# A transformer block on one Trainium2 core: the output projection adds PSUM to its own partial sums, with three steps put in another order

## The chip, the cores and the metric

The kernel runs on one core of one Trainium2 chip. The metric is the time of one execution on the device, in microseconds (us), of that core. Five engines appear in the profile: TensorE (PE, with its weight loads as PEld), VectorE (DVE), ScalarE (ACT), GpSimd (POOL) and SyncE (SP), which here only issues DMAs. [...]

## The reference

The input x has 32 sequences of 64 tokens and 1024 features, float32. The reference computes

```python
x = x + attn(cond(x))     # cond: x @ W.T plus a rank-32 term chosen per sequence
x = x + ffn(cond2(x))     # two layers of 8 gated rank-16 experts beside a dense product
```

where `attn` is causal attention with 32 query heads, 8 key and value heads of width 32, rotary positions, and an output projection `out @ w_o.T + b_o` with a 1024 x 1024 weight. Only `w_o`, its bias and the sum with x are touched by the larger part of the change.

## The kernel before, in words

**The two stages.** The weights of consecutive layers are first multiplied with each other (`multiply`, L530): the chain called cq multiplies `w1` into the query weights, then ckv, then cf. After about 297 us the tokens are done in two halves of 1024 (`for hf in range(2)`, L766): query and key products, scores and values, output projection, and then the feed-forward part. Both halves run the same code, so each stage around the change comes twice.

**The products.** A product of a 256-column weight chunk with 1024 columns is a `Group` (L220): a 2 x 2 block scheme with seven block products in place of eight. It needs sums of weight blocks (`weight_sums`, L163, on POOL) and sums of columns (`column_sums`, L176, on DVE, called t1 to t4 below). The seven steps are p1, p6, p5, p7, p2, p4 and p3, on three PSUM banks: x (p1, then p2), y (p6, then p7, then p4) and z (p5, then p3). Three partial sums go to SBUF tiles: p1 is copied by ACT (L273), and two DVE additions follow p6 (L279, "u1") and p7 (L291, "u2"). A step that accumulates onto a bank has to wait until the partial result before it has been read from there: p7 until u1 is read from y, p4 until u2 is read from y, p3 until the result called out11 is read from z. The four results of a group are out11, out00, out10 and out01, in the order in which their products end.

**The output projection.** `o_pairs` (L1011) makes its groups. `known` (L1018) is called as soon as each of the three partial sums exists and lets POOL add it to x; `out_o` (L1022) then lets DVE add the PSUM bank to x, in the same x tile, so that this DVE instruction (L1026, or L1028 without a bias) waits for the POOL instruction (L1020) that was given to x before it. Half of the projection (G = 0, four groups) is done between the attention units u = 4 to 7; the other half (G = 1) follows in two pairs.

**The attention units.** A unit u has four score tiles. `scores` (L873) makes them on PE, `masked` (L899) lets DVE add the mask into a tile e, `maxima` (L908) takes row maxima on DVE and subtracts them on POOL (L913), `normalised` (L915) lets ACT take exponentials, DVE sum them and take reciprocals (L922, L923), and POOL multiply (L925). `turned` (L927) transposes e on PE, and `values` (L939) multiplies with v.

**What sets the order.** Within `tc.manual_schedule()` (L1034) the order of each engine's queue is the order of the calls in the code. In the loop at L1092 an iteration for u is: transposes, p1, `normalised(u + 1)` (after p6 if u is 4), the scores of unit u + 2, p6, their four mask additions, p5, p2, p7, two maxima, the values, out11, p4, two maxima, p3. In the loop at L1038, which goes on with the query products beside the first two units, an iteration is p1, p6, `masked(u)` (which makes its scores first), p5, and so on. Outside of such a block (the feed-forward part, which begins at L1142) a planner with estimated costs picks the order from what it expects to be ready.

**The first loads.** SP issues the first loads of chain cq at L568 to L576: for the first half of the inner dimension the weight chunk `w0`, four chunks of `wq` with `b1` after the first, then `w1`; then the same for the second half. The first product needs `w0[:, :4, :128]` and the first 512 columns of `wq` for chunks 0 to 3. DVE makes t1 and t2 chunk by chunk in turn, then t3 (L579).

Of the kernel before, what the change touches and what calls it, by code (L numbers as in the profile page):

```python
# [16 lines left out]
ALU = mybir.AluOpType  # L17
AX = mybir.AxisListType

P = 128  # L20
D = 1024
KC = D // P
B, S = 32, 64
# [53 lines left out]
def block_kernel(ctx: ExitStack, tc: tile.TileContext, a, out: bass.AP):  # L77
    nc = tc.nc
# [27 lines left out]
    mask = cst[:, _C["mask"]]  # L106
# [19 lines left out]
    bqk, bo, bb = biases[:, 0:10], biases[:, 10 : 10 + KC], biases[:, 10 + KC :]  # L126
# [31 lines left out]
    H = KC // 2  # L158

    def by_sequence(m):  # L160
        return m.rearrange("p (b t) -> p b t", t=S)
# [311 lines left out]
    with tc.tile_pool(name="gen", bufs=1) as gen:  # L473
# [87 lines left out]
        wq = gen.tile([P, KC, D], F32, tag="right", name="wq")  # L561
# [3 lines left out]
        b1 = gen.tile([P, KC, LR], F32, tag="b1", name="b1")  # L565
        w0, w1 = (wp.tile([P, KC, WG], F32, tag="w", name=f"w_cq{g}") for g in range(2))
        first_half, second_half = slice(0, H), slice(H, KC)
        for half in (first_half, second_half):  # L568
            nc.sync.dma_start(w0[:, half], a["w1"][0, :, half])
            for kc in range(half.start, half.stop):  # L570
                nc.sync.dma_start(wq[:, kc, :], a["wqkv"][:, kc, :D])
                if kc == 0:
                    nc.sync.dma_start(b1, a["b1"])
            nc.sync.dma_start(w1[:, half], a["w1"][1, :, half])
        nc.sync.dma_start(index, a["index"])
        nc.sync.dma_start(cst, a["consts"])  # L576
        b1q_rows = rank_rows("b1q", b1, wq, D, b1q)
        t_cq = columns("cq", gen, halves(wq, D), 512)
        for which in ((0, 1), (2,)):  # L579
            for kc in range(H):  # L580
                t_cq.make(kc, which)
        t_ckv, make_ckv = sums_of("ckv", wkv, NQ - D)
        t_cf, make_cf = sums_of("cf", w3, D)

# [181 lines left out]
    for hf in range(2):  # L766
# [3 lines left out]
        def x_half(kc, c, x=x):  # L770
            return x[kc].rearrange("p (b c t) -> p b c t", c=2, t=S)[:, :, c, :]
# [101 lines left out]
        def scores(u):  # L873
            g, b0 = u // 4, u % 4 * 4
            sc = [ps_tile(f"sc_{hf}_{u}_{j}") for j in range(4)]
            for n in range(8):
                mp, b = n // 4, b0 + n % 4
                for j in range(4):
                    rows = slice(j * HD, (j + 1) * HD)
                    nc.tensor.matmul(  # L880
                        sc[j][:, n * S : (n + 1) * S],
                        q[rows, g, b, 2 * mp : 2 * mp + 2, :].rearrange("p m t -> p (m t)"),
                        k[rows, g, b, :],
                        start=True,
                        stop=True,
                    )
            return sc
# [3 lines left out]
        units = {}  # L891

        def per_key(v):
            return v.rearrange("p (n t) -> p n t", t=S)
# [1 line left out]
        def wide(v):  # L896
            return v.unsqueeze(2).to_broadcast([P, 8, S])

        def masked(u, sc=None):  # L899
            units[u] = []  # L900
            for j, sc in enumerate(sc or scores(u)):
                e = ep.tile([P, 512], F32, tag="e", name=f"e_{hf}_{u}_{j}")
                nc.vector.tensor_add(  # L903
                    per_key(e), per_key(sc), mask.unsqueeze(1).to_broadcast([P, 8, S])
                )
                units[u].append(e)

        def maxima(u, js=range(4)):  # L908
            for j in js:
# [99 lines left out]
                column_sums(tiles, lambda i, c: b(i, c, kcs), cols)  # L1009

        def o_pairs(G, p, ws, t, banks):  # L1011
            nm = f"o{hf}{G}{p}"
            w, s = ws

            def group(i):
                g = 2 * p + i

                def known(r, c, add):  # L1018
                    xo = x_half(g + r * H, c)
                    nc.gpsimd.tensor_add(xo, xo, by_sequence(add))  # L1020

                def out_o(r, c, ps, add):  # L1022
                    xo = x_half(g + r * H, c)
                    if G == 0:
                        bias = bo[:, g + r * H : g + r * H + 1]
                        nc.vector.scalar_tensor_tensor(xo, by_sequence(ps), bias, xo, ALU.add, ALU.add)  # L1026
                    else:
                        nc.vector.tensor_add(xo, by_sequence(ps), xo)  # L1028

                return Group(f"{nm}{i}", w[:, i], s[:, i], t, out_o, None, known, banks[i])  # L1030

            return [group(i) for i in range(2)]

        with tc.manual_schedule():  # L1034

            rotated()
            pair, held = qk_pair(2), None
            for u in range(2):  # L1038
                g = pair
                g.p1()  # L1040
                g.p6()
                masked(u)
                g.p5()
                maxima(u)
                g.p7()
                g.p2()
                normalised(u)
                g.together(held)
                if u == 0:
                    held, pair = g, qk_pair(3, ps_tile)  # L1050
                else:
                    wv = load_w(cqkv[:, :, 5 * WG :], f"v{hf}")
                g.p4()
                g.p3()
            g.last_rows()
            v_ranks(0, 1)
            g.out01()
            v_mult(0)
            rotated()
            pools.close()  # L1060
            wsp = scoped(f"ws{hf}", 4)
            sums = scoped(f"sums_o{hf}")
            t0 = [sums.tile([P, 2, 512], F32, tag=f"sum{j}", name=f"sum{j}_o{hf}0") for j in range(4)]
            v_out(0)
            for u in range(4):
                first, second = 2 * u + 1, 2 * u + 2
                ws = turned(u)
                if u > 0:
                    normalised(u + 1)
                v_mult(first)  # L1070
                v_out(first)
                if 0 < u < 3:
                    o_sums(0, t0, u - 1, u)
                masked(u + 2)
                if u == 3:
                    values(u, ws, group_bank)
                    o_sums(0, t0, u - 1, u + 1)
                    maxima(u + 2)
                    break
                v_ranks(second, second + 1)  # L1080
                v_mult(second)
                maxima(u + 2)
                v_out(second)
                values(u, ws)
                if u == 0:
                    wo0 = o_load(0, 0)

            wo1 = o_load(0, 1)
            ot = Columns(o_columns(0), 512, 2, [[t[:, kc, :] for kc in range(2)] for t in t0])
            pairs = o_pairs(0, 0, wo0, ot, (group_bank, group_bank))  # L1090
            pairs += o_pairs(0, 1, wo1, ot, (group_bank, group_bank))
            for u in range(4, 8):  # L1092
                o = pairs[u - 4]
                ws = turned(u)
                o.p1()
                if 4 < u < 7:
                    normalised(u + 1)
                elif u == 7:
                    t1 = [
                        [ep.tile([P, 512], F32, tag="e", name=f"sumo{hf}{j}{kc}") for kc in range(2)]  # L1100
                        for j in range(4)
                    ]
                    o_sums(1, t1, 4, 7)
                sc = scores(u + 2) if u < 6 else None
                o.p6()
                if u == 4:
                    normalised(u + 1)
                if u < 6:
                    masked(u + 2, sc)
                o.p5()  # L1110
                o.p2()
                o.p7()
                if u < 6:
                    maxima(u + 2, range(2))
                if u == 6:
                    wo0 = o_load(1, 0)
                values(u, ws)
                o.out11()
                o.p4()
                if u < 6:  # L1120
                    maxima(u + 2, range(2, 4))
                o.p3()
            o_sums(1, t1, 7, 8)
            ot = Columns(o_columns(1), 512, 2, t1)
            wo1 = o_load(1, 1)
            pairs = o_pairs(1, 0, wo0, ot, (group_bank, ps_tile))
            pools.close()

            xt = columns(f"y{hf}", scoped(f"sums_y{hf}", side="right"), x_half, 512)
            for p in range(2):  # L1130
                for step in ("p1", "p6", "p5", "p7", "p2", "out11", "p4", "p3"):
                    for o in pairs:
                        getattr(o, step)()
                    if p == 1 and step in ("p5", "out11"):
                        xt.make(("p5", "out11").index(step))
                pairs = o_pairs(1, 1, wo1, ot, (group_bank, ps_tile))
            attention.close()
# [209 lines left out]
```

## Time and profile before

| what | value |
|---|---|
| time, median of 3 runs | 1225.39 us (1225.35 to 1227.83) |
| time of the profiled execution | 1223.48 us |
| its span, first to last instruction | 1221.7 us |
| around the span | 1.78 us |
| granted TensorE clock | 0.999 |
| busy: PE, DVE, POOL, ACT | 98%, 47%, 42%, 13% |
| output projection beside units 4 to 7, first half of the tokens | 482.41 to 548.13 us |
| the same, second half | 946.99 to 1012.69 us |

Times inside the trace count from the first instruction of the profiled execution. A line of a timeline gives the start, the duration, the engine, the source line, the operation with its output and inputs, how many were merged, and in brackets how long the engine was idle before it and what ended that. [...] products of four times two 512-column passes start 3.43 us apart although each shows 3.60 us, so stalls are read from start to start.

### The profile page before, as it was taken

How to read it: one execution, taken by the hardware profiler on the slowest of the kernel's cores; microseconds unless marked ns; L12 is line 12 of the kernel's file. 1: busy time of each engine (PE TensorE's matmuls, PEld its weight loads, DVE VectorE, ACT ScalarE, POOL GpSimd, SP SyncE). 2: the span in 40 equal slices, each digit the busy share in tenths (PEclk: the TensorE clock that was granted, in tenths of full speed). 3: DMA queues.
4: the chain of work that ended last, by engine and by line, in shares of the span. 5: the costliest groups of instructions: out<-in, count | busy, mean ns of one | idle time of the engine just before them, and what ended most of it. 6: DMA issues, size and time to landing. Idle time of an engine off the chain costs nothing.

```text
span 1221.7 us, 13568 instructions
## 1 busy us (share of the span) xinstructions
PE 1202.3 (98%) x5434; PEld 610.6 (50%) x5434; DVE 574.8 (47%) x940; ACT 153.5 (13%) x282; POOL 510.2 (42%) x437
## 2 busy tenths in 40 slices
PE   7999999999999999999999999999999999999998
PEld 2444875555444477444444444444478444444443
DVE  4312151115358789753942113457789764743111
ACT  1001000000001125320000000001124330000000
POOL 3441361443435646734726011533656752821010
PEclk9999999999999999999999999999999999999999
DMA  6563732644111111013114235111111023212110
GB/s 241 201 221 101 269 131 70 207 152 157 35 34 36 37 68 70 21 67 122 35 35 138 69 107 169 35 35 35 35 70 38 34 70 101 73 35 69 50 55 35
DMA packets 57504, 108.83 MB, mean 89 GB/s; under 512 B 5088, under 2 KB 34144, under 8 KB 56160
## 3 DMA queue, kind: packets, MB, share of 16 engines
q1 hardware_dynamic: 41648, 79.53, 19.5%
q10 hardware_dynamic: 13104, 20.03, 4.5%
q0 software_dynamic: 2688, 8.39, 2.0%
q8 instruction: 43, 0.70, 0.2%
q14 instruction: 21, 0.17, 0.0%
HBM read 83.72 MB, written 24.22 MB: 88 GB/s over the span
## 4 chain that ended last, share of the span: by engine, by line
PE 91%; DVE 4%; POOL 3%; issue 1%; DMA 0%; ACT 0%; SPq 0%; POOLq 0%; DVEq 0%; ACTq 0%
PE qk_y L249 7%; PE f_y L249 7%; PE o_y L249 5%; PE qk_z L249 5%; PE qk_x L249 5%; PE v L859 5%; PE f_z L249 5%; PE f_x L249 4%; PE o_z L249 4%; PE o_x L249 4%; PE cq_y L249 3%; PE cf_y L249 3%; PE cq_x L249 2%; PE cf_x L249 2%; PE cq_z L249 2%; PE cf_z L249 2%
## 5 line engine op out<-in xcount | busy, mean ns | idle before, releaser
L809 POOL TENSOR_TENSOR raw<-raw,consts 128x512 f32<-128x512 f32 x40 | 63.1, 1585 | 105.9 <-DVE t L808 105.9
L913 POOL TENSOR_TENSOR e<-e,top 128x512 f32<-128x512 f32 x64 | 64.9, 1042 | 55.4 <-DVE top L912 40.4
L925 POOL TENSOR_TENSOR e<-e,tot 128x512 f32<-128x512 f32 x64 | 66.2, 1064 | 20.0 <-DVE tot L923 20.0
L249 PE MATMUL qk_x<-x,w_qk 128*128 128x512 f32 x160 | 72.2, 594 | 0.0
L249 PE MATMUL qk_y<-sum_x,s_qk 128*128 128x512 f32 x160 | 72.0, 593 | 0.0
L170 POOL TENSOR_TENSOR s_f<-w_f 128x512 f32<-128x512 f32 x8 | 11.0, 1379 | 123.0 <-DMA w_f<-cffn 99.4
L249 PE MATMUL o_x<-q,w_o 128*128 128x512 f32 x128 | 58.9, 592 | 0.0
L859 PE MATMUL v<-w_v,x 128*128 128x256 f32 x256 | 58.7, 382 | 0.0
L249 PE MATMUL f_x<-x,w_f 128*128 128x512 f32 x128 | 57.9, 592 | 0.0
L249 PE MATMUL f_y<-sum_y,s_f 128*128 128x512 f32 x128 | 57.5, 592 | 0.0
L922 DVE TENSOR_REDUCE tot<-e 128x8 f32<-128x512 f32 x64 | 40.2, 665 | 25.4 <-ACT e L917 25.2
L859 PEld LDWEIGHTS v<-w_v,x 128*128 128x128 f32 x256 | 47.4, 190 | 8.4 <-issue 2.7
L1020 POOL TENSOR_TENSOR x<-x,o_u 128x512 f32<-128x512 f32 x32 | 42.0, 1322 | 22.7 <-DVE o_u L291 18.4
L249 PEld LDWEIGHTS qk_y<-sum_x,s_qk 128*128 128x128 f32 x160 | 30.3, 190 | 37.9 <-issue 37.5
L249 PEld LDWEIGHTS qk_x<-x,w_qk 128*128 128x128 f32 x160 | 30.1, 190 | 38.0 <-issue 37.9
L810 DVE TENSOR_TENSOR t<-t,consts 128x512 f32<-128x512 f32 x40 | 47.3, 1194 | 0.7
L170 POOL TENSOR_TENSOR s_qk<-w_qk 128x512 f32<-128x512 f32 x10 | 18.5, 1851 | 66.6 <-DMA w_qk<-cqkv 66.6
L917 ACT ACTIVATE e<-e 128x512 f32<-128x512 f32 x64 | 38.2, 640 | 48.9 <-POOL e L913 48.9
L903 DVE TENSOR_TENSOR e<-sc,consts 128x512 f32<-128x512 f32 x64 | 39.5, 678 | 3.2 <-PE sc L880 3.2
L249 PEld LDWEIGHTS f_y<-sum_y,s_f 128*128 128x128 f32 x128 | 24.3, 190 | 30.6 <-issue 30.6
L249 PEld LDWEIGHTS f_x<-x,w_f 128*128 128x128 f32 x128 | 24.3, 190 | 30.6 <-issue 30.6
L912 DVE TENSOR_REDUCE top<-e 128x8 f32<-128x512 f32 x64 | 39.6, 674 | 0.0
(314 smaller groups left out, 2187.9 us busy)
## 6 DMA issues: line engine op xcount, KB each, us to landing
w_qk<-cqkv SPq DMA_DIRECT2D x10, 1024.0 KB, 6.4
x<-in_xT SPq DMA_DIRECT2D x16, 512.0 KB, 7.5
w_o<-in_wo SPq DMA_DIRECT2D x16, 512.0 KB, 5.1
s_o<-wos SPq DMA_DIRECT2D x16, 512.0 KB, 6.5
w_f<-cffn SPq DMA_DIRECT2D x8, 1024.0 KB, 5.6
outT<-o ACTq DMA_DIRECT2D x32, 256.0 KB, 2.4
wq<-in_wqkv SPq DMA_DIRECT2D x8, 512.0 KB, 8.9
cqkv<-cq ACTq DMA_DIRECT2D x16, 256.0 KB, 3.8
```

Source lines behind the costliest of these rows:

```text
L170: nc.gpsimd.tensor_add(s[:, 0], a21, a22)
L249: nc.tensor.matmul(ps, self.weights[left][:, kc, :], self.right(right, kc), start=first and kc == 0, stop=kc == self.h - 1, skip_group_che ...
L809: nc.gpsimd.tensor_mul(rv, rv, c3)
L810: nc.vector.tensor_mul(t2v, t2v, s3)
L859: nc.tensor.matmul(begun[t], x[kc][:, t * P : (t + 1) * P], wv[:, kc, :], start=False, stop=kc == KC - 1, skip_group_check=True,)
L903: nc.vector.tensor_add(per_key(e), per_key(sc), mask.unsqueeze(1).to_broadcast([P, 8, S]))
L912: nc.vector.tensor_reduce(top, ev, AX.X, ALU.max)
L913: nc.gpsimd.tensor_sub(ev, ev, wide(top))
L917: nc.scalar.activation(e, e, AF.Exp, scale=SCALE)
L922: nc.vector.tensor_reduce(tot[:, i], es[i], AX.X, ALU.add)
L925: nc.gpsimd.tensor_mul(es[i], es[i], wide(tot[:, i]))
L1020: nc.gpsimd.tensor_add(xo, xo, by_sequence(add))
```

## The change

Four edits.

1. In `o_pairs`, for all groups but the last pair (`last`), DVE adds the PSUM bank (and the bias where G is 0) to the partial sum's own tile, and POOL then adds that tile to x. The three POOL additions of `known` go away there; three POOL additions after out11, out10 and out01 come in. out00, which has no partial sum, still goes straight to x on DVE.
2. In the loop over u = 4 to 7, `normalised(u + 1)` stands behind p6 for every u. Two of the four mask additions move behind p5 and p7, p7 comes ahead of p2, and out11 comes directly behind the mask additions, ahead of the values.
3. In the loop over u = 0 and 1, for u = 0 p5 comes ahead of the scores.
4. The first load of `w0` and the first of `wq` are each split into two by columns, and the first column halves of both are issued first; `b1` follows, and the second half of `w0` stands behind `w1`. DVE makes all of t1, then all of t2, then all of t3.

```diff
-        for half in (first_half, second_half):
-            nc.sync.dma_start(w0[:, half], a["w1"][0, :, half])
-            for kc in range(half.start, half.stop):
+        for r in range(2):
+            cols, outs = slice(r * D // 2, (r + 1) * D // 2), slice(r * P, (r + 1) * P)
+            nc.sync.dma_start(w0[:, first_half, outs], a["w1"][0, :, first_half, outs])
+            nc.sync.dma_start(wq[:, 0, cols], a["wqkv"][:, 0, cols])
+        nc.sync.dma_start(b1, a["b1"])
+        for half in (first_half, second_half):
+            for kc in range(max(half.start, 1), half.stop):
                 nc.sync.dma_start(wq[:, kc, :], a["wqkv"][:, kc, :D])
-                if kc == 0:
-                    nc.sync.dma_start(b1, a["b1"])
             nc.sync.dma_start(w1[:, half], a["w1"][1, :, half])
+            if half is first_half:
+                nc.sync.dma_start(w0[:, second_half], a["w1"][0, :, second_half])
...
-        for which in ((0, 1), (2,)):
+        for j in range(3):
             for kc in range(H):
-                t_cq.make(kc, which)
+                t_cq.make(kc, (j,))
...
+            last = (G, p) == (1, 1)
...
                 def known(r, c, add):
-                    xo = x_half(g + r * H, c)
-                    nc.gpsimd.tensor_add(xo, xo, by_sequence(add))
+                    if last:
+                        xo = x_half(g + r * H, c)
+                        nc.gpsimd.tensor_add(xo, xo, by_sequence(add))
...
                 def out_o(r, c, ps, add):
                     xo = x_half(g + r * H, c)
+                    bias = bo[:, g + r * H : g + r * H + 1]
+                    to, more = (xo, xo) if last or add is None else (by_sequence(add), by_sequence(add))
                     if G == 0:
-                        bias = bo[:, g + r * H : g + r * H + 1]
-                        nc.vector.scalar_tensor_tensor(xo, by_sequence(ps), bias, xo, ALU.add, ALU.add)
+                        nc.vector.scalar_tensor_tensor(to, by_sequence(ps), bias, more, ALU.add, ALU.add)
                     else:
-                        nc.vector.tensor_add(xo, by_sequence(ps), xo)
+                        nc.vector.tensor_add(to, by_sequence(ps), more)
+                    if to is not xo:
+                        nc.gpsimd.tensor_add(xo, xo, to)
...
-                masked(u)
-                g.p5()
+                if u == 0:
+                    g.p5()
+                    masked(u)
+                else:
+                    masked(u)
+                    g.p5()
...
-                if 4 < u < 7:
-                    normalised(u + 1)
-                elif u == 7:
+                if u == 7:
...
                 o.p6()
-                if u == 4:
+                if u < 7:
                     normalised(u + 1)
                 if u < 6:
-                    masked(u + 2, sc)
+                    masked(u + 2, sc, range(2))
                 o.p5()
+                o.p7()
+                if u < 6:
+                    masked(u + 2, sc, range(2, 4))
+                o.out11()
                 o.p2()
-                o.p7()
                 if u < 6:
                     maxima(u + 2, range(2))
...
                 values(u, ws)
-                o.out11()
                 o.p4()
```

`masked` takes a list of score tiles to be done (`js`), so that a unit's four mask additions can be issued in two calls.

## The prediction, on record before the changed kernel ran

> **What bounds the kernel now.** I read the page's busy times and chain first, then the list of whom TensorE waits for, then TensorE's timeline in the stages that the change touches, then DVE and POOL beside it.
>
> ```profile
> PE 1202.3 (98%) x5434; PEld 610.6 (50%) x5434; DVE 574.8 (47%) x940; ACT 153.5 (13%) x282; POOL 510.2 (42%) x437
> ...
> PE 91%; DVE 4%; POOL 3%; issue 1%; DMA 0%; ACT 0%; SPq 0%; POOLq 0%; DVEq 0%; ACTq 0%
> ```
>
> TensorE is busy nearly throughout and holds 91% of the chain that ended last. No matmul is added or removed, so all that can be won is the time in which TensorE waits. The list of its waits (total, times, longest):
>
> ```profile
> PE cq_x L249 <- DMA wq<-in_wqkv: 7.4, 1, 7.4
> PE o_y L249 <- DVE o_u L291: 2.3, 2, 1.2
> PE o_z L249 <- DVE x L1026: 1.9, 4, 0.5
> PE sc L880 <- DVE q L819: 1.1, 2, 0.5
> ```
>
> Edits 1 and 2 aim at the second and third line, edit 3 at the fourth, edit 4 at the first. TensorE in unit 4 of the first half (p7, values, p4, p3, transposes):
>
> ```profile
> 491.42 1.88 PE L249 MATMUL o_y<-sum_o,s_o 128*128 128x512 f32 x4
> 493.23 1.09 PE L948 MATMUL av<-ws,v 64*32 64x256 f32 x32
> 495.49 1.98 PE L249 MATMUL o_y<-sum_o,w_o 128*128 128x512 f32 x4 [1.16 <-DVE o_u L291]
> 498.00 1.98 PE L249 MATMUL o_z<-q,s_o 128*128 128x512 f32 x4 [0.54 <-DVE x L1026]
> 499.82 1.91 PE L933 MATMUL pt<-consts,e 128*128 128x128 f32 x16
> ```
>
> The pitch of an unhindered half product is 1.72 us (487.99 to 489.70), and 1.03 us from values to the next (512.39 to 513.41, unit 5). So p4 could start at 494.26 and started 1.23 later; p3 could start 1.81 behind p4 (1.72 and about 0.1 after a restart) and started 2.51 behind, 0.70 late. DVE shows why:
>
> ```profile
> 488.25 0.69 DVE L279 TENSOR_TENSOR o_u<-o_y,o_p 128x512 f32<-128x512 f32 x1 [1.20 <-PE o_y L249]
> ...
> 491.75 2.42 DVE L903 TENSOR_TENSOR e<-sc,consts 128x512 f32<-128x512 f32 x4
> 494.09 0.74 DVE L1026 SCALAR_TENSOR_TENSOR x<-o_x,consts,x 128x512 f32<-128x512 f32 x1
> 494.75 0.68 DVE L291 TENSOR_TENSOR o_u<-o_y,o_p 128x512 f32<-128x512 f32 x1
> ...
> 497.20 0.75 DVE L1026 SCALAR_TENSOR_TENSOR x<-o_z,consts,x 128x512 f32<-128x512 f32 x1 [0.58 <-POOL x L1020]
> ```
>
> u2 (L291), which frees y for p4, stands behind four mask additions and a result; out11 (last line), which frees z for p3, waits for POOL. POOL's queue:
>
> ```profile
> 490.66 1.27 POOL L1020 TENSOR_TENSOR x<-x,o_u 128x512 f32<-128x512 f32 x1
> 491.89 4.05 POOL L925 TENSOR_TENSOR e<-e,tot 128x512 f32<-128x512 f32 x4
> 495.89 1.27 POOL L1020 TENSOR_TENSOR x<-x,o_u 128x512 f32<-128x512 f32 x1
> ```
>
> The addition of u2 to x, for which out11 waits, sits behind four multiplications. The scores of unit 0, against those of unit 1, which nothing hinders:
>
> ```profile
> 380.68 1.34 PE L880 MATMUL sc<-k,q 32*128 32x64 f32 x40
> 382.56 0.90 PE L880 MATMUL sc<-k,q 32*128 32x64 f32 x24 [0.55 <-DVE q L819]
> 383.39 3.70 PE L249 MATMUL qk_z<-sum_x,s_qk 128*128 128x512 f32 x8
> ...
> 408.88 2.01 PE L880 MATMUL sc<-k,q 32*128 32x64 f32 x64
> 410.83 3.70 PE L249 MATMUL qk_z<-sum_x,s_qk 128*128 128x512 f32 x8
> ```
>
> 2.71 against 1.95 us to the next product: 0.76 lost.
>
> [...] the column sums L182 to L188 of two SBUF tensors take 0.69 us alone and up to 1.75 beside POOL, while L1026, with a PSUM input, took 0.75 beside POOL's multiplications. [...] the DVE addition from PSUM stays in both versions; every POOL row here reads SBUF. [...] The first product agrees: its matmuls start 0.85 us apart until about 11 us, then 0.43. [...] here two loads with 512 B rows (w_h, 572.5 to 574.5 us) ran at 275 and 347 GB/s against 413 later[...].
>
> **Edits 1 and 2, units 4 to 7.** Stalls before, start to start, p4 and p3: unit 4 1.23 and 0.70; unit 5 0 and 0.25 (513.41 to 515.38 less 1.72); unit 6 0 and 0.70; unit 7 0 and 0.24. Sum 3.12 a half; the second half has the same starts to 0.05 (p4 960.07, p3 962.57, 979.95, 995.64, 1010.87). 6.2 us in all.
>
> What is left is DVE's queue in the new order, from the start S of p6. From the trace: u1 starts at S + 2.09 (486.16 to 488.25) and takes 0.61 of pitch; four sums and two reciprocals take 2.89 (488.86 to 491.75); two mask additions 1.2; u2 0.69. So u2 ends at S + 7.5. TensorE reaches p4 at S + 8.1 (the same steps, with p7 now third): 0.6 to spare. Two more mask additions (1.2) and out11 (0.75) end at S + 9.35; p3 comes at S + 9.92: 0.55 to spare. p7, moved up, starts at S + 3.55 and needs u1, done at S + 2.8. The values' second bank needs only the first mask addition, done about S + 6.2, and comes at S + 7.1. [...] The exponentials, which ended before S + 4 in unit 4, come no later; ACT has nothing else to do between p1's copy and them; in units 5 and 6 DVE no longer waits for them (3.86 idle before L922) ahead of u1.
>
> POOL: three additions of 1.27 go, three come; out11 no longer waits for POOL. Its queue per unit stays 8 x 1.03 + 3 x 1.27 = 12.1 us in a unit of 15.3 or 17.2. The multiplications that the next transposes need end about S + 8.5 (first reciprocal S + 4.3, then 4.05), the transposes come at S + 11.65 (p4 at 8.1, p3 1.82 and the transposes 1.75 behind it): 3.2 to spare. Behind POOL's new additions stand the subtractions for the unit after the next, with 2 us or more of slack to the exponentials. In unit 7 eight column sums (5.2 us in the trace, one POOL addition beside them) run ahead of u1; p7 comes 1.7 earlier now. Unit 6's last result leaves DVE 1 us after unit 7's first transpose starts, the sums end 6.2 after it, u1 6.9; p7 comes at 6.95. That is no slack: I charge 0.1 to 0.6 a half, taking 0.2. The pair (1, 0) loses and gains nothing: TensorE ran there without a gap (548.13 to 596.29), and x for the following column sums is ready 5 us ahead.
>
> Gain 6.2 - 0.4 = 5.8 us; bounds 5.0 and 6.4 (0.1 more at a restart that disappears).
>
> **Edit 3.** q's last piece came at 382.5; with p5 first the scores start near 384.1, so 0.76 goes in each half: 1.5 us. The mask additions, maxima (2.45) and exponentials come 3.4 later; DVE ends the sums of unit 0 near 395.1, where out11 started at 395.11 before, and p3, which waits for it, comes only near 397.7. The price is nothing, at worst 0.3 a half.
>
> **Edit 4.** Before, w0 was used at 5.85, the first product began at 7.36, at the cold pitch, and the fourth chunk came by 11.56; the product ended near 13.0. The bytes ahead of the fourth chunk are the same, moved at about 410 GB/s, so it lands no earlier. TensorE can start its first chunk near 6.0, then waits for the second (8.92). At most the 0.4 us between landing and use of the fourth is won. Against it: 512 KB in 512 B rows, estimated from the w_h rates at 0 to 0.6 us; and an idle gap of 1.2 us in the warm-up, which may keep the half clock for longer[...]. SP issues three more DMAs of 0.45 us, while transfers are queued ahead. t2 and t3 are ready before p6 (27.25) and p7 in either order. I take 0.1 us lost, from -0.4 to +1.7. The 7.4 us before the first matmul shrink in the list but not in the span.
>
> **The sum.** 5.8 + 1.5 - 0.1 = 7.2, less 0.1 for the planner's order behind the stage, which may shift by a few tenths either way: 7.1 us. The profiled execution took 1223.48 us (span 1221.7 and 1.78 around it) and would take 1216.4; it was 1.91 below the median, for which I expect 1225.39 - 7.1 = 1218.3.
>
> **Rivals.**
> (a) The start costs: the half clock stays and the rows of 512 B cost. 1.5 lost: 1219.8. [...] against it: TensorE has something to do from 9 us on.
> (b) DVE is tighter than I reckon: half of the stalls come back at p7 of unit 7 or p4 of unit 5, 3 us: 1221.4. For it: slacks of 0 to 0.6; against it: the durations come from the same forms in the same neighbourhood.
> (c) Slower: POOL's multiplications, now behind u1, end after the transposes need them. They have 3.2 us; each microsecond beyond that is paid in units 5 to 7 of both halves, six times. From 4.4 late on the gain is gone, from 4.8 on it is slower; at 5 late 10.8 is lost: 1229.1. For it: POOL works in order and waits for DVE; against it: 12.1 us of work in 15.3.
> (d) The edits free TensorE of nothing, because the waits of the list only hide others: 1225. Against it: the pitches in units without stalls are measured.
>
> **Chances.** Forecast 0.70, (a) 0.12, (b) 0.08, (c) 0.05, (d) 0.05. About 0.2% (2.45 us) is what a measurement of this kernel can tell from no change: below 1222.9 is faster. That gives faster 0.88 (forecast, a, most of b), same 0.07, slower 0.05. The range runs from 1216.3 (bounds 6.4 and 1.5, 0.4 won at the start, and 0.8 of spread between runs) to 1221.8 (b).
>
> **What would show it.** In the new trace TensorE's list has no o_y <- L291 and at most hundredths for o_z; unit 4's transposes to unit 5's are 2 us closer; the scores of unit 0 take 1.95; out11 no longer waits for POOL; the first product starts near 6 and ends near 13. A wait of pt for POOL L925, or of o_y for L279 in unit 7 above 0.6, would make the prediction wrong.

## The result, and the profile after

The changed kernel takes 1216.82 us (median of 6 runs, 1215.41 to 1220.74) against 1225.7 for the kernel before (6 runs): a ratio of 0.9927, interval [0.9909, 0.9946]. Measured once more later it is 0.9935 [0.9917, 0.9953]. The gain is 7 to 9 us where 7.1 was forecast, and the time lies in the range given. The profiled execution after took 1215.41 us with a span of 1213.6, 8.1 less than before. Its busy times and its chain, from the page:

```profile
PE 1200.8 (99%) x5434; PEld 611.3 (50%) x5434; DVE 577.8 (48%) x940; ACT 153.7 (13%) x282; POOL 511.1 (42%) x437
...
PE 99%; DMA 0%; SPq 0%; DVE 0%; issue 0%; DVEq 0%
```

The work of each engine is what it was; DVE and POOL have left the chain. All that TensorE still waits for (total, times, longest):

```profile
PE cq_x L249 <- DMA wq<-in_wqkv: 7.1, 2, 4.7
PE cq_y L249 <- DVE cq_u L291: 0.8, 1, 0.8
PE f_z L249 <- issue: 0.6, 1, 0.6
PE h L429 <- issue: 0.2, 1, 0.2
```

The lines o_y <- L291, o_z <- L1026 and sc <- L819 are gone. TensorE in unit 4 of the first half, now in the order p7, p2, values, p4, p3, transposes:

```profile
489.87 1.88 PE L249 MATMUL o_y<-sum_o,s_o 128*128 128x512 f32 x4
491.58 1.88 PE L249 MATMUL o_x<-q,w_o 128*128 128x512 f32 x4
493.39 1.09 PE L953 MATMUL av<-ws,v 64*32 64x256 f32 x32
494.42 1.98 PE L249 MATMUL o_y<-sum_o,w_o 128*128 128x512 f32 x4
496.24 1.88 PE L249 MATMUL o_z<-q,s_o 128*128 128x512 f32 x4
497.96 1.91 PE L938 MATMUL pt<-consts,e 128*128 128x128 f32 x16
```

No step is later than its pitch: p4 starts 1.03 after the values, p3 1.82 after p4. DVE beside it (p6 starts at S = 486.33):

```profile
488.42 0.69 DVE L279 TENSOR_TENSOR o_u<-o_y,o_p 128x512 f32<-128x512 f32 x1 [1.20 <-PE o_y L249]
...
491.93 1.22 DVE L908 TENSOR_TENSOR e<-sc,consts 128x512 f32<-128x512 f32 x2
493.06 0.68 DVE L291 TENSOR_TENSOR o_u<-o_y,o_p 128x512 f32<-128x512 f32 x1
493.66 1.28 DVE L908 TENSOR_TENSOR e<-sc,consts 128x512 f32<-128x512 f32 x2
494.86 0.74 DVE L1035 SCALAR_TENSOR_TENSOR o_u<-o_z,consts,o_u 128x512 f32<-128x512 f32 x1
```

Two mask additions instead of four and a result stand ahead of u2 (L291); it ends at S + 7.41, 0.7 ahead of p4. out11 (last line) has no idle time ahead of it: it reads PSUM and its own partial sum, and POOL comes afterwards:

```profile
490.73 4.05 POOL L930 TENSOR_TENSOR e<-e,tot 128x512 f32<-128x512 f32 x4 [1.10 <-DVE tot L928]
495.74 1.27 POOL L1039 TENSOR_TENSOR x<-x,o_u 128x512 f32<-128x512 f32 x1 [0.96 <-DVE o_u L1035]
```

The four multiplications still come first, but now only POOL's own addition stands behind them. The scores of unit 0:

```profile
383.66 1.45 PE L249 MATMUL qk_z<-sum_x,s_qk 128*128 128x512 f32 x3
385.04 2.01 PE L885 MATMUL sc<-k,q 32*128 32x64 f32 x64
386.98 3.70 PE L249 MATMUL qk_y<-sum_x,s_qk 128*128 128x512 f32 x8
```

1.94 to the next product, in one piece. Only the start of the program is not as wished:

```profile
4.67 2.05 PE L249 MATMUL cq_x<-wq,w_cq 128*128 128x512 f32 x2 [4.67 <-DMA wq<-in_wqkv]
9.15 4.78 PE L249 MATMUL cq_x<-wq,w_cq 128*128 128x512 f32 x6 [2.44 <-DMA wq<-in_wqkv]
13.87 1.92 PE L503 MATMUL b1q<-wq,b 128*32 128x512 f32 x16
```

TensorE starts 2.7 us earlier, then waits 2.44 for the second chunk. Its matmuls start 0.85 us apart up to the last but one (12.73), twice the 0.43 of full clock; this is called the half clock below. b1q, the work behind the product, starts at 13.87 where it started at 12.94.

**Where the 8.1 us come from**, start to start, both halves together, before against after:

| stretch | difference, us |
|---|---|
| first product up to the one behind b1q (start at 14.79, 15.72) | +0.93 |
| scores of unit 0 (2.71, 1.94) | -1.5 |
| unit 4's transposes to the first product of the pair (1, 0) (67.52, 64.29) | -6.46 |
| wait of h_x for ACT, missing after | -0.26 |
| wait f_z <- issue, first half (1.30, 0.63) | -0.66 |
| rest | -0.1 |

h_x and f_z are PSUM banks of groups in the feed-forward part, which the change doesn't touch.

### The profile page after: what moved, and what is told of

Read it like the earlier page. It is cut to its first block, busy times and chain, and to the rows that moved or that the text cites. A ratio compares the mean times of both kernels' runs of the same rounds, so it can differ in the third digit from the quotient of the medians.

```text
span 1213.6 us, 13600 instructions
## 1 busy us (share of the span) xinstructions
PE 1200.8 (99%) x5434; PEld 611.3 (50%) x5434; DVE 577.8 (48%) x940; ACT 153.7 (13%) x282; POOL 511.1 (42%) x437
## 4 chain that ended last, share of the span: by engine, by line
PE 99%; DMA 0%; SPq 0%; DVE 0%; issue 0%; DVEq 0%
PE qk_y L249 9%; PE o_y L249 7%; PE f_y L249 7%; PE qk_x L249 6%; PE qk_z L249 6%; PE v L864 5%; PE f_z L249 5%; PE o_x L249 5%; PE o_z L249 5%; PE f_x L249 5%; PE cq_y L249 3%; PE cf_y L249 3%; PE sc L885 3%; PE cq_x L249 2%; PE pt L938 2%; PE cf_z L249 2%
## 5 line engine op out<-in xcount | busy, mean ns | idle before, releaser
L170 POOL TENSOR_TENSOR s_f<-w_f 128x512 f32<-128x512 f32 x8 | 11.5, 1437 | 121.2 <-DMA w_f<-cffn 97.4
L1039 POOL TENSOR_TENSOR x<-x,o_u 128x512 f32<-128x512 f32 x24 | 30.9, 1291 | 54.3 <-DVE o_u L1037 33.2
```

Source lines behind the costliest of these rows:

```text
L1039: nc.gpsimd.tensor_add(xo, xo, to)
```

## The experiments

My theory: edits 1 and 2 remove the whole of the 3.1 us of stalls a half only together, edit 3 removes 0.76 a half, and edit 4 is worth nothing or less. Rivals: one of the two edits does it alone; the start gains; a new queue takes some back. Measured beside the first four experiments the kernel before took 1228.84 us (median), beside the next four 1222.82, beside the last four 1228.65; so ratios are compared, and stages of the traces. "The stage" is the stretch from unit 4's transposes to the first product of the pair (1, 0), in the first half.

**Edit 4 undone** (e1). The loads and the order of t1 to t3 as before, all else changed:

```diff
-        for r in range(2):
-            cols, outs = slice(r * D // 2, (r + 1) * D // 2), slice(r * P, (r + 1) * P)
...
-        for j in range(3):
+        for which in ((0, 1), (2,)):
```

> The changed kernel with edit 4 undone (first loads and order of t1 to t3 as before). My theory: edit 4 costs, because TensorE starts at 4.7 us, idles from 6.7 to 9.2 and so stays at half clock for longer. Then the second part of the first product's after-work (b1q) starts near 12.9 us as in the kernel before and not at 13.9, and the time is about 0.9 us below the changed kernel's 1216.8: near 1216. Rival: how long the half clock lasts is chance from run to run, and edit 4 is worth nothing either way: b1q anywhere from 12.5 to 14, time near 1216.8. Second rival: the early start pays in most runs and only the profiled one was unlucky: time near 1218.

1219.97 us, ratio 0.9924 [0.9911, 0.9937], the same as with edit 4 as far as an interval of 1.6 us to either side can tell. The stage takes 64.29, the scores 1.94. The gain is there without edit 4. b1q starts at 13.71, not near 12.9 as my theory had it: the trace goes with the rival that calls the length of the half clock chance.

**Edit 4 alone** (e2), the same lines put into the kernel before.

> The kernel before with edit 4 alone. My theory: b1q starts near 13.9 us and not at 12.9, the rest of the trace is the kernel before's moved by 0.9, time near 1226.6. Rival (chance): time near 1225.7, b1q anywhere from 12.5 to 14. Second rival (the early start pays): 1224.5.

1228.43 us, ratio 0.9995 [0.9984, 1.0006]: no gain; the interval reaches from 2.0 won to 0.7 lost. b1q starts at 14.26. Over all profiled executions without added matmuls it starts at 12.94, 13.79, 13.71, 13.42 and 13.33 with the old loads and at 13.87, 14.26, 13.88, 13.85, 14.38 and 14.01 with the new ones: means of 13.44 and 14.04. The two sets don't overlap, though by 0.06 us only. Edit 4 costs some 0.6 us in the traces; the times can't tell that from nothing.

**Edit 2 alone** (e3): the order of the loop over u = 4 to 7, with POOL still adding to x ahead of the results.

> The kernel before with edit 2 alone (the order of the loop over units 4 to 7), POOL still adding each partial sum to x. The stage from unit 4's first transpose to the first product of the pair (1, 0) takes 67.5 us before and 64.3 in the changed kernel. My theory: p4 no longer waits, but out11 now stands earlier on DVE and still waits for POOL's addition behind the four multiplications, so p3 waits 1.8 in unit 4, 0.65 in unit 5, 0.55 in unit 6: the stage takes about 67.3, the time is near 1225.3. Rival: the order is what pays and POOL's wait is a trifle: stage 65, time near 1220.5.

1228.46 us, ratio 0.9998 [0.999, 1.0006]. The stage takes 67.72 instead of 67.52. TensorE's waits and POOL's queue in this kernel:

```profile
PE o_z L249 <- DVE x L1026: 5.3, 6, 1.8
```

```profile
492.33 4.05 POOL L925 TENSOR_TENSOR e<-e,tot 128x512 f32<-128x512 f32 x4
496.34 1.26 POOL L1020 TENSOR_TENSOR x<-x,o_u 128x512 f32<-128x512 f32 x1
```

o_y <- L291 is gone, and its time is back at o_z, now up to 1.75 at once: out11 still waits for POOL's addition, which stands behind the multiplications (4.05), so p3 comes when it can, whatever the order ahead of it.

**Edit 1 alone** (e4): the sums added the other way, the order as before.

> The kernel before with edit 1 alone (DVE adds PSUM to the partial sums, POOL adds those to x), in the old order. My theory: all waits of p3 for out11 go (1.9 us a half), the 1.23 of p4 in unit 4 stays, since there u2 stands behind four mask additions: the stage takes 65.6 in place of 67.5, time near 1221.9. Rival: POOL's additions behind the results stand in front of the subtractions in POOL's queue and make the exponentials late: stage 67 or more, time 1225 or more.

1222.48 us, ratio 0.9954 [0.9937, 0.9972]; the stage takes 65.65 (65.6 expected), 1.87 less a half. By the medians the time fell by 6.4 us where 3.8 were expected (the interval reaches from 3.4 to 7.7), which the stage doesn't show. The six runs fall into two groups: 1220.78 to 1222.88 at a granted clock of 0.999 or 1.0, and 1226.18 and 1226.76 at 0.997; the last section tells what goes with such a difference of the clock. The waits of the projection that are left:

```profile
PE o_y L249 <- DVE o_u L291: 2.3, 2, 1.2
```

So edit 1 is worth 1.9 a half alone and edit 2 nothing alone (0.2 lost), but together they win 3.23: edit 2 is worth 1.4 a half once edit 1 is in.

**Edit 3 alone** (e5), in the kernel before:

```diff
-                masked(u)
-                g.p5()
+                if u == 0:
+                    g.p5()
+                    masked(u)
+                else:
+                    masked(u)
+                    g.p5()
```

> The kernel before with edit 3 alone (the fifth product ahead of the first scores). If the wait of the first scores for q is what edit 3 removes, and nothing is given back at the mask additions, maxima or exponentials behind it, the scores of unit 0 take 1.95 us instead of 2.71, in both halves, and the kernel gains 1.5 us: a ratio near 0.9988. Rival: the wait only moves to the exponentials or to p3 of the pair, and the ratio is 1.000.

1221.07 us (18 runs), ratio 0.9984 [0.9977, 0.9991]: 1.1 to 2.8 us won. The scores take 1.94 (384.97 to 386.91), and nothing new is in TensorE's list. The theory holds.

**The normalising back ahead of p6** (e6), units 5 and 6:

```diff
                 o.p1()
-                if u == 7:
+                if 4 < u < 7:
+                    normalised(u + 1)
+                elif u == 7:
...
                 o.p6()
-                if u < 7:
+                if u == 4:
                     normalised(u + 1)
```

> The changed kernel with the normalising of the next unit put back ahead of the sixth product in units 5 and 6 (as before the change), everything else left. The theory that DVE's queue up to the first sum decides: the four sums and reciprocals (2.9 us) then stand ahead of u1, which p7 needs 3.55 us after p6 starts; p7 stalls about 1.1 us in each of the two units, 2.2 a half, 4.4 us in all, a ratio to the kernel before near 0.9965 where the changed kernel has 0.993. Rival: the sums are done before p6's sum is ready, the place of the normalising costs nothing, and the time is that of the changed kernel.

1218.93 us, ratio 0.9964 [0.995, 0.9977]. The mechanism is there, in one unit of the two. Unit 5's p6 and p7 have no gap: DVE began to sum at 502.77, and u1 ended at 506.31, 0.7 ahead of p7. In unit 6 no scores stand ahead of p6, so that it comes earlier while DVE waits 3.73 for the exponentials; p7 then waits:

```profile
523.49 1.99 PE L249 MATMUL o_y<-sum_o,s_o 128*128 128x512 f32 x4 [1.34 <-DVE o_u L279]
```

That is 2.7 us of waiting in both halves, and 3.2 in the stage (65.89 instead of 64.29 a half), instead of the 4.4 expected. The ratio is near the 0.9965 expected, but the changed kernel, from which the 4.4 were reckoned, was not measured beside it.

**TensorE busy ahead of the first product**, with the new loads (e7) and with the old ones (e8):

```diff
+        warm = tmp("warm")
+        nc.vector.memset(warm, 1.0)
+        idle = ps_tile("idle")
+        for _ in range(4):
+            nc.tensor.matmul(idle, warm[:, :P], warm, start=True, stop=True)
```

> The changed kernel with four added matmuls on a constant tile ahead of the first product, whose result nothing uses; they run while the first loads are still under way. The theory that the half clock (a matmul pitch of 0.85 us instead of 0.43 in the whole first product) is what keeps the first product's end at 13.9 us: with TensorE busy ahead of it, the clock is full when the chunks come, the product ends near 13.0 and the kernel gains 0.9 us over the changed kernel (a ratio to before of 0.992 instead of 0.993). Rival: the arrival of the third and fourth chunk decides, the product ends near 13.5 at best, and the gain is under 0.4 us.

> The changed kernel with edit 4 undone (the loads of the start as before) and the same four added matmuls, whose result nothing uses. The theory of the half clock: the first product ends near 12.5 us, about 1 us earlier than without the added matmuls, and this is the fastest of the versions (a ratio to before near 0.9915). Rival: the chunks' landing decides, and it is within 0.4 us of the changed kernel with the old loads.

1214.21 us, ratio 0.9924 [0.9909, 0.9939], and 1213.95 us, ratio 0.9921 [0.9905, 0.9936]. The start in e7:

```profile
7.19 1.02 PE L249 MATMUL cq_x<-wq,w_cq 128*128 128x512 f32 x2
9.09 1.12 PE L249 MATMUL cq_x<-wq,w_cq 128*128 128x512 f32 x2 [0.88 <-DMA wq<-in_wqkv]
10.37 1.13 PE L249 MATMUL cq_x<-wq,w_cq 128*128 128x512 f32 x2 [0.16 <-DMA wq<-in_wqkv]
11.67 1.12 PE L249 MATMUL cq_x<-wq,w_cq 128*128 128x512 f32 x2 [0.17 <-DMA wq<-in_wqkv]
12.72 1.92 PE L503 MATMUL b1q<-wq,b 128*32 128x512 f32 x16
```

Two matmuls of a chunk take about 1.1 us and TensorE waits for each chunk: b1q starts 1.15 earlier than with the change (e8: 12.61). So in the changed kernel the half clock was the bound, and with full clock the chunks' landing is. The times don't show it yet: e8's ratio of 0.9921 stands against 0.9924 for the same loads without the added matmuls (e1), within the 0.4 us of its rival.

**The changed kernel, with and without the added matmuls, on one chip** (c1 and c2).

> The changed kernel itself once more, so that the next three can be held against it on one chip. The stages gain 6.5 (edits 1 and 2) and 1.5 us (edit 3) and the start loses or wins less than 0.9: a ratio between 0.9928 and 0.9942. If the larger gain of the first measurement (8.9 us) was due to the wait ahead of the first feed-forward group, whose size differed between executions, the ratio is nearer to 0.9935 here; if the change itself shortens that wait, it stays at 0.9927.

> The changed kernel with four added matmuls ahead of the first product, whose result nothing uses, beside the changed kernel on one chip. The theory of the half clock: about 1.1 us less than the changed kernel in the same call, as the product's end in the trace (12.72 instead of 13.87 us). Rival: what the start wins is lost again in later waits, and the two are within 0.4 us.

1221.42 us (1218.02 to 1223.36), ratio 0.9935 [0.9917, 0.9953], and 1219.84 (1218.69 to 1222.09), ratio 0.9923 [0.991, 0.9936]. c1's ratio is the one expected if the first measurement's larger gain was chance; its interval holds the 0.9927 as well. The medians of c1 and c2 differ by 1.6, the ranges overlap: inconclusive. The profiled execution of c2 even shows the opposite of e7's:

```profile
6.59 1.02 PE L249 MATMUL cq_x<-wq,w_cq 128*128 128x512 f32 x2
9.74 1.12 PE L249 MATMUL cq_x<-wq,w_cq 128*128 128x512 f32 x2 [2.14 <-DMA wq<-in_wqkv]
11.04 3.35 PE L249 MATMUL cq_x<-wq,w_cq 128*128 128x512 f32 x4 [0.17 <-DMA wq<-in_wqkv]
14.31 2.20 PE L503 MATMUL b1q<-wq,b 128*32 128x512 f32 x16
```

The second chunk came 0.65 us later than in e7, TensorE stood for 2.14 instead of 0.88, and from 11.5 us on it ran at half clock again. With the new loads the early first chunk makes that gap; with the old ones (e8) no gap is over 0.5 us.

**POOL's slack** (e9 and e10): two and four additions, whose result nothing uses, ahead of the multiplications for units 5, 6 and 7:

```diff
+                if u > 4 and two == 0:
+                    spare = tmp(f"spare_{hf}_{u}")
+                    for _ in range(2):
+                        nc.gpsimd.tensor_add(spare, es[0].rearrange("p n t -> p (n t)"), es[1].rearrange("p n t -> p (n t)"))
```

> The changed kernel with two spare two-input additions on POOL (1.27 us each, the result used by nothing) ahead of the multiplications in units 5, 6 and 7. The slack of 3.2 us between the end of the multiplications and the transposes: 2.5 us later costs nothing at the transposes; at worst the subtractions behind, with some 2 us of slack, let the exponentials come late in unit 5, 0.5 us a half. Ratio to the changed kernel 1.000 to 1.001. Rival: POOL decides already, each addition is paid six times, 15 us in all, a ratio of 1.012.

> The changed kernel with four such spare additions at the same place, 5.1 us. The slack of 3.2 us: the transposes wait 1.9 us for the multiplications in each of units 5, 6 and 7, in both halves, some 11 us in all, a ratio to the changed kernel near 1.009; with that the gain is gone, as the rival of the prediction that ends slower reckoned. Rival: POOL's slack is larger than reckoned (over 5 us), and the ratio is 1.000; or it is none, and the ratio is 1.025.

With two: 1216.92 us (4 runs), ratio 0.992 [0.9891, 0.995]; the stage takes 64.29, as in c1 (480.74 to 545.03). With four: 1226.88, ratio 0.9983 [0.997, 0.9997] against c1's 0.9935; the stage takes 67.92. TensorE's waits in it:

```profile
PE pt L942 <- POOL e L934: 3.3, 6, 0.7
...
PE o_y L249 <- DVE o_u L279: 1.5, 2, 0.8
```

All six waits of the transposes are those of unit 7, three in each half; POOL's multiplications for units 6 and 7 ahead of them:

```profile
512.23 4.05 POOL L934 TENSOR_TENSOR e<-e,tot 128x512 f32<-128x512 f32 x4
...
529.33 4.67 POOL L934 TENSOR_TENSOR e<-e,tot 128x512 f32<-128x512 f32 x4
```

```profile
530.43 0.66 PE L942 MATMUL pt<-consts,e 128*128 128x128 f32 x4
531.43 0.66 PE L942 MATMUL pt<-consts,e 128*128 128x128 f32 x4 [0.34 <-POOL e L934]
532.74 0.65 PE L942 MATMUL pt<-consts,e 128*128 128x128 f32 x4 [0.66 <-POOL e L934]
534.06 0.65 PE L942 MATMUL pt<-consts,e 128*128 128x128 f32 x4 [0.66 <-POOL e L934]
```

POOL's multiplications for unit 6 ended at 516.28 where the transposes began at 515.22, and none waited: each of the four steps needs only its own tile, so the last is due over a microsecond after the first. For unit 7 they start at 529.33 (522.81 in c1), and every tile is late.

How much slack this shows has to be read from how late the multiplications came, not from the time added. Counted back from the transposes they start 7.23 us ahead in c1 in each of the three units. In e9 the added work fell mostly into time in which POOL had waited, and they were 1.6, 0.0 and 0.4 later; so e9 tests little of the slack. In e10 they were 4.3 and 4.2 later in units 5 and 6, at no cost, and 6.3 later in unit 7 (against a start of the transposes 15.0 behind unit 6's, as in c1), where POOL's queue had fallen further behind. The slack is at least 4.2 us and less than 6.3: the 3.2 reckoned, and the microsecond and more by which the last tile is due later. Beyond it the stage loses 3.6 us a half, not the 5.7 expected, as only one unit of the three is late.

## Why the prediction was right

The stages and the start sum to 7.05 us in the profiled pair (6.46 + 1.52 - 0.93) where the prediction had 7.2 for them. That it is so near is in part luck: edits 1 and 2 gave 0.66 more than forecast, and edit 4 took 0.83 more.

**Edits 1 and 2** (forecast 5.8): 6.46 in the profiled pair, 3.23 a half, just beyond the upper bound of 6.4. The sum of stalls, 3.12 a half, has two small errors that nearly cancel. p3 starts 1.82 behind p4 also where nothing waits (494.42 to 496.24 after), so that three of its four stalls were counted 0.1 too big; and the step behind a stalled p3 came 1.82 later instead of 1.72 (498.00 to 499.82 before, 496.24 to 497.96 after), 0.1 in each of the four units, which the sum left out. 2.82 of stalls and 0.4 make 3.22. The reckoning of DVE's queue held: u2 at S + 7.41 (7.5), out11 ends at S + 9.27 (9.35). The charge of 0.2 a half in unit 7 did not fall due: there u1 ends at 536.67 and p7 comes at 536.97. One column sum (L184, from 531.52, two SBUF inputs) took 1.51 beside POOL's addition, which itself took 1.52 (from 531.10); the seven other column sums of unit 7 took 0.54 to 0.56. The addition with a PSUM input (L1035) took 0.74 with POOL's addition beside it (from 495.51) as without (494.86). What the prediction did not say: the two edits are worth more together than apart (0, 1.9, 3.2 a half), because with edit 2 alone p4 comes earlier and p3 then waits all the longer for POOL's addition, and with edit 1 alone p4 still waits for u2.

**Edit 3** (1.5): 0.77 and 0.77; right.

**Edit 4** (0.1 lost, bounds 0.4 won to 1.7 lost, the second bound the author's estimate): the right sign, the size too small. Lost: 0.93 in the profiled pair, 0.6 as a mean of eleven traces. The step that failed is "TensorE can start its first chunk near 6.0, then waits for the second (8.92)": it started at 4.67, so that the gap was not 1.2 but 2.44, and the half clock lasted until 13.09, where before it ended at 11.34 (the trace keeps the moments at which the granted clock changes). The 11.34 is luck of the kernel before's trace: over the five traces with the old loads it is 11.34 to 12.99, over the six with the new ones 12.55 to 13.84. The product ended near 13.9, not near 13: what rival (a) described, at 0.6 to 0.9 of the 1.5 us estimated there. The second chunk landed later as well: its first matmul starts at 9.15, at 9.21 to 9.67 in the other five traces, where its weights could be loaded at 8.92 before; 314 GB/s were moved from 7.5 to 9 us, at a DMA share of 1.00, and 423 before. How much each of the two costs was not tried apart.

**The order behind the stage** (0.1 won): 0.9 in the profiled pair, from two waits in the first half. h_x's wait for ACT (0.26) is in the lists of the kernel before, e2, e3 and e5, and in none with edit 1. The other, f_z, is chance: see the last section. They are why this pair shows 8.1 where the stages and the start sum to 7.05.

**The rivals.** (b) and (d) are excluded by the waits that are gone. (c) was given 3.2 us of slack: in c1 the multiplications end at 526.86 and the transposes start at 530.04, 3.2 again, and 4.2 or more counted tile by tile (e10). Its price was too high: it assumed that unit 5's and unit 6's transposes are late with unit 7's.

**The fastest version** run is the changed kernel with the old loads and the added matmuls (e8): 1213.95 us against 1222.82 for the kernel before measured beside it, level with e7 (1214.21). It was not run beside the changed kernel itself; that it beats it is read from the start in the traces (12.61 against 13.85 to 14.38), not from times.

## What to carry to other kernels

When two engines update the same tile one after the other, look for the side that the critical engine waits for, and let that side finish without the other: here DVE frees the PSUM bank with its own partial sum, and POOL's addition comes when it comes. Of two causes of a stall one can show nothing when it alone is removed (edit 2: nothing alone, 1.4 us a half behind edit 1), so try such edits together before dropping one. An early start of TensorE at the head of a program is worth something only if the work then goes on: started 2.7 us earlier and then idle for 2.4, it ended later.

## What the runs showed of the hardware

**Waits of 2.27 to 3.71 us brought the half clock back in five runs, and then cost 1.7 to 1.8 us more.** In the feed-forward part of the first half TensorE's p3 waits for DVE's out11 (L1228), of which the profile can't tell what held it. The changed kernel in c1, and the same place in e7:

```profile
652.73 1.02 PE L264 MATMUL f_y<-hwr,b2f 128*128 128x512 f32 x2
657.28 5.40 PE L249 MATMUL f_z<-x,s_f 128*128 128x512 f32 x8 [3.52 <-issue]
```

```profile
651.64 1.02 PE L264 MATMUL f_y<-hwr,b2f 128*128 128x512 f32 x2
652.50 3.61 PE L249 MATMUL f_z<-x,s_f 128*128 128x512 f32 x8
```

After 3.52 us of waiting the product takes 5.40 instead of 3.61: 5.3 us in all. The half clock came back after waits of 3.48 to 3.71 us (e1, e2, c1, c2: products of 5.29 to 5.40) and after the shorter 2.27 too (e10: 5.40), and not after 2.31 and 2.75 (e3, e4: 3.70). What tells these apart in the traces is where the wait lies. The moments at which the granted clock changes are whole multiples of 3.4133 us apart: 354 of them lie between the changes at 11.34 and 1219.66 in the kernel before, 352 between those at 13.09 and 1214.59 in the changed one. The stretch of this grid that holds most of the wait, and the next one, in e10 and in e4 (PEclk is the granted clock):

```profile
core 0: us, PE busy (x) PEld busy (x) DVE busy (x) ACT busy (x) POOL busy (x), PEclk, DMA share, GB/s
658.24:661.65 3.41, 1.14 (x4) 0.62 (x4) 0.75 (x1) 0.00 (x0) 1.90 (x2) 1.00 0.38 96
661.65:665.07 3.42, 3.42 (x6) 1.36 (x5) 0.00 (x0) 0.69 (x1) 0.00 (x0) 0.50 0.48 172
```

```profile
653.97:657.38 3.41, 1.40 (x4) 0.33 (x2) 0.49 (x2) 0.00 (x0) 2.54 (x3) 1.00 0.78 250
657.38:660.80 3.42, 2.68 (x7) 1.25 (x7) 0.69 (x1) 0.69 (x1) 0.95 (x1) 1.00 0.60 189
```

TensorE was busy for 1.14 us of the stretch in e10, and PEclk is 0.50 for the whole of the next; likewise behind 0.00 (e2), 0.38 (c1), 0.65 (c2) and 0.95 (e1). Behind 1.40 (e4) and 1.54 (e3) it stays 1.00, although e4's wait is the longer one: it lies across two stretches. No sharp limit is shown: at the start of c2 the half clock followed on 1.61 us of work in short pieces.

**The same wait differs from execution to execution, and the kernel doesn't explain it:** 1.30 (before), 0.63 (after), 3.48, 3.69, 2.31 and 2.75 (e1 to e4), none in e5 to e8, 3.52, 3.71, 1.35 and 2.27 (c1, c2, e9, e10). It goes more with what was measured together than with the kernel. The kernel before's medians, 1228.84 beside e1 to e4, 1222.82 beside e5 to e8 and 1228.65 beside the last four, go with it; the 6 us between them are about what the wait and the half clock behind it cost. So do the six runs of c1: 1218.02 and 1218.29 us at a granted clock of 1.000 and 0.999, 1220.04 to 1223.36 at 0.998 and 0.997. Beside the wait run sixteen gathers of POOL, which the second half, where the wait is absent, doesn't have; but they run in e5 to e8 too. A load of 1 MB runs there in both halves. Whether the gathers hold DVE back was not tried, and the cause stays open.
